# Semantic rows of the first layer's stacks: from DMA transfers to ScalarE copies

## The chip, the cores and the metric

The kernel runs on one core of one Trainium2 chip. The metric is the time of one execution on the device in microseconds (us), as the median of several runs; lower is better. In the profile PE is TensorE's matmuls, PEld its weight loads, DVE is VectorE, ACT is ScalarE, POOL is GpSimd, SP is the engine that issues most transfers. ACTq and SPq are the instruction queues of ScalarE and SP, in which a transfer's issue shows up.

## What is computed

Two cross-attention layers run one after the other on 16 sequences of 256 positions with 320 channels (20 heads of 16). Each attends to a context of 256 rows, of which the first 77 are text and the other 179 are image tokens in layer 0. The first layer (layer 0 in the code) is the one that the change touches. Cut to what matters:

```
logits     = q_h @ k_h^T * scale                    # per head, 77 text keys
text_out   = softmax(logits) @ v_h
scores     = q_h @ ip_k_h^T * scale                 # per head, 179 image keys
text_probs = softmax(q @ k_text^T * scale)          # all heads together: 77 columns
sem        = (text_probs @ text) @ ip^T * scale
fused      = scores + 0.5 * sem                     # the same sem in every head
ip_out     = (softmax(fused) * spatial_mask) @ ip_v_h
out        = (text_out + ip_out) @ Wout + bout + x
```

So the semantic term is a product of a 77-row matrix (text_probs, transposed) with a 77 x 179 matrix (half of text times ip), added to the scores of every head.

## The kernel before, in words

**Stacks.** The kernel adds the semantic term by stacking rows along the contraction dimension of one matmul. A stack is a pair of tiles Q and K, each 128 partitions x 4 heads x 256. There are four such pairs (`SIZES["NR"]`), used in turn by step k; a step is one group of four heads of one sequence, five steps a sequence, 80 steps in layer 0 (`NS`). Before the change rows 0 to 47 (`XROW` = 48) hold q and k in three parts of 16 rows (high halves and remainders of the numbers), rows 48 to 124 the 77 semantic rows, and rows 125 and 126 (`KS0` = 127) serve to subtract the row maxima: K holds there two rows of -1 (one for the text columns, one for the image columns), and Q the row maxima themselves. In K the semantic rows are zero for the 77 text columns (set once, by a memset).

**Filling a stack** is `stacks0` (L608 to L622). Four transfers go through the helper `dma`, which issues on SP (L82): part "K" and part "Q" bring 48 rows from DRAM (`kd<-kst` and `qd<-q` wrote them there); part "T" broadcasts `tph` (the transposed text probabilities, 77 x 256) to the four heads, and part "M" broadcasts the 77 x 179 matrix `M`. Parts T and M are done for groups 0 to 3 of a sequence only, because group 4 uses the same pair as group 0 and finds them there. The stack of step k + 4 (`LEAD`) is filled in step k, once the matmuls of step k that read the same pair are issued.

**A step of layer 0** is `slot0`. In order it asks for `maxima0` of step k + 1, the first half of `score0` of step k + 2, the first half of `turned0` of step k, `attend0` of step k - 1, and then the second halves of `score0` and `turned0`; between them stands work of other parts (projections of queries, keys and values, the close of a sequence), which a list of tasks with due times hands out. TensorE keeps this written order (`PINNED`). The order on ScalarE, VectorE, GpSimd and SP is made by the framework's scheduler in the loop; in the ramp before it (`begin`) all engines keep the written order.

**The maxima.** `score0` makes the scores of four heads (L649) and reduces them on VectorE to two maxima a head, over text (L650) and image columns (L651), into `mn`. `maxima0` turns `mn` with a matmul (L657), copies the result to `mt`, 8 rows x 256, on ScalarE (L659), and brings it into rows 125 and 126 of Q by one transfer for each head, issued on ScalarE (L661; on SP for the first two steps). `turned0` makes the scores again, transposed and with the maxima subtracted (L673), takes the exponential on ScalarE (L676) and multiplies on GpSimd by `rs`, a factor from the second-order part of the semantic term (L679). The second exponential of a step is ordered behind the issue of the next step's last maxima transfer. `values0` multiplies with the values (L709), and `settle0` normalizes.

**The semantic softmax** is `semantic0`, once a sequence: matmuls (L571), a copy on ScalarE (L573), the row maximum on VectorE, the exponential with its sum on ScalarE (L582), then the reciprocal (L585) and the scaling (L586) on VectorE, for two halves of 128 positions; then a transpose on TensorE (L590), and `tph` as a high half (L592, ScalarE) and a remainder (L593).

Of the kernel before, what the change touches and what calls it, by code (L numbers as in the profile page):

```python
# [9 lines left out]
FR = mybir.dt.float32r  # L10
AF = mybir.ActivationFunctionType
ALU = mybir.AluOpType
AX = mybir.AxisListType
# [4 lines left out]
S = 256  # L18
# [5 lines left out]
T0 = 77  # L24
# [7 lines left out]
KS0 = 127  # L32
KS1 = 50
XROW = 48
# [14 lines left out]
def xattn2(  # L49
# [27 lines left out]
    nc = tc.nc  # L77
    f = lambda ap: ap.bitcast(F32)
    mm = nc.tensor.matmul

    def dma(out, in_):
        nc.sync.dma_start(*(f(ap) if ap.dtype == FR else ap for ap in (out, in_)))  # L82
# [16 lines left out]
    def buf(tag, shape, dtype=F32, bufs=1, name=None):  # L99
        if tag in ("wB", "wD", "vr", "raw"):  # L100
            return sb.tile(shape, dtype, tag=tag, name=name or tag, bufs=bufs)
        size = 1
        for d in shape[1:]:
            size *= d
        if tag not in slots:
            slots[tag] = [0, dtype] + [const_tile([128, max(size, words.get(tag, 0))], f"{tag}_{i}", dtype) for i in range(bufs)]
        n, kind, *ring = slots[tag]
        assert kind == dtype and len(ring) == bufs, tag
        slots[tag][0] += 1
        t = ring[n % bufs][: shape[0], :size]  # L110
        names = "abcd"[: len(shape) - 1]
        if len(names) > 1:
            t = t.rearrange(f"p ({' '.join(names)}) -> p {' '.join(names)}", **dict(zip(names, shape[1:])))
        return t
# [4 lines left out]
    kd = [dram.tile([B // 2, 3, CP, 2, S], F32, name="kd0"), dram.tile([B, 3, CP, 1, S], F32, name="kd1")]  # L119
# [21 lines left out]
    def anchor(inst):  # L141
        anchors[inst.ins.engine] = inst
        return inst
# [120 lines left out]
    for i in range(SIZES["NR"]):  # L264
        nc.gpsimd.memset(f(ks[i]), 0.0)
        nc.gpsimd.memset(f(qs[i]), 0.0)
        dma(ks[i][XROW + T0 : KS0], ind0r.unsqueeze(1).to_broadcast([2, 4, S]))
    V0W, V1W = 17, 22
    vr = [buf("vr", [128, 3, H * V0W + 16], bufs=3) for i in range(3)]
    vcols = lambda v, w: v[:, :, : H * w].rearrange("p t (h e) -> p t h e", e=w)  # L270
# [268 lines left out]
    def stack_rows(d):  # L539
        return d.rearrange("r (d h) t -> (r d) h t", h=HP)  # L540
# [13 lines left out]
    def semantic0(b):  # L554

        qh, qd = get("q0", b)
        NT = 96
        kt = first_kt[0] if b == 0 else buf("kb", [128, 3, 2, NT], FR, name="kt")
        for s, r in ((0, 0), (1, 2)) if b else ():
            dma(kt[:, :, s], kd[0][b // 2, r].rearrange("(m p) b t -> p m b t", p=128)[:, :, b % 2, :NT])  # L560
        yield
        mh = get("m0t", b)

        tps = []
        for t in range(2):
            sf = bank()
            for k in range(3):
                qt = lambda h: qh[:, h, k, t * 128 : (t + 1) * 128]
                for h in range(2):
                    both = kt[:, k].rearrange("p s n -> p (s n)")  # L570
                    mm(sf[:, : 2 * NT], qt(h), both, start=k + h == 0, stop=k + h == 3)  # L571
            sp = buf("sp", [128, T0], bufs=2)
            nc.scalar.copy(sp, sf[:, NT : NT + T0])  # L573
            nc.vector.tensor_add(sp, sp, sf[:, :T0])
            mz = buf("mx", [128, 2], bufs=2)
            mx, zs = mz[:, 0:1], mz[:, 1:2]
            nc.vector.tensor_reduce(mx, sp, axis=AX.X, op=ALU.max)
            nc.vector.tensor_scalar_mul(mx, mx, -SCALE)
            tps.append((sp, mx, sp, zs))
            yield  # L580
        for sp, mx, tp, zs in tps:
            nc.scalar.activation(tp, sp, AF.Exp, bias=mx, scale=SCALE, accum_out=zs)  # L582
        yield
        for sp, mx, tp, zs in tps:
            nc.vector.reciprocal(zs, zs)  # L585
            nc.vector.tensor_scalar_mul(tp, tp, zs)  # L586
        yield
        tpp = bank()
        for t in range(2):
            nc.tensor.transpose(tpp[:T0, t * 128 : (t + 1) * 128], tps[t][2], ident)  # L590
        tph = buf("tph", [T0, 2, S], FR, bufs=2)
        nc.scalar.copy(tph[:, 0], tpp[:T0, :S])  # L592
        nc.vector.tensor_sub(tph[:, 1], tpp[:T0, :S], f(tph[:, 0]))  # L593
        yield

        rs = buf("rs", [128, 2, S], bufs=2)
        rp = bank().rearrange("p (t q) -> p t q", t=2)
        for t in range(2):
            mm(rp[:, t], mh[:, 0, t * 128 : (t + 1) * 128], tph[:, 1], start=True, stop=False)
            mm(rp[:, t], mh[:, 1, t * 128 : (t + 1) * 128], tph[:, 0], start=False, stop=True)  # L600
        nc.scalar.activation(rs, rp, AF.Exp, scale=SCALE)
        yield
        return qd, tph, rs, mh
# [4 lines left out]
    def stacks0(k, parts="KQTM"):  # L608
        b, g = divmod(k, NG)
        Q, K = QK[k] = qs[k % SIZES["NR"]], ks[k % SIZES["NR"]]  # L610
        hs = slice(4 * g, 4 * g + 4)
        for part in parts:
            if part == "K":
                dma(K[0:XROW], stack_rows(kd[0][b // 2][:, :, b % 2])[:, hs])
            elif part == "Q":
                dma(Q[0:XROW], stack_rows(get("q0", b)[1])[:, hs])
            elif g < SIZES["NR"]:
                tph, mh = get("s0", b)[1::2] if part == "T" else (None, get("m0t", b))
                if part == "T":
                    dma(Q[XROW : XROW + T0], tph[:, 0:1].to_broadcast([T0, 4, S]))  # L620
                else:
                    dma(K[XROW : XROW + T0, :, T0:], mh[:, 0:1, T0:].to_broadcast([T0, 4, S - T0]))  # L622


    def stacks1(k):
# [16 lines left out]
    def score0(k, t):  # L642
        Q, K = QK[k]
        if t == 0:
            maxes[k] = buf("mn", [128, 2, 4, 2], FR, bufs=2)
        mn = maxes[k]
        sp = scores()
        for h in range(4):
            mm(sp[:, h], Q[: XROW + T0, h, t * 128 : (t + 1) * 128], K[: XROW + T0, h], start=True, stop=True)  # L649
        nc.vector.tensor_reduce(mn[:, t, :, 0], sp[:, :, :T0], axis=AX.X, op=ALU.max)  # L650
        anchor(nc.vector.tensor_reduce(mn[:, t, :, 1], sp[:, :, T0:], axis=AX.X, op=ALU.max))  # L651

    def maxima0(k, queue=nc.scalar):
        Q, mn = QK[k][0], maxes[k]
        mp = bank()
        for t in range(2):
            mm(mp[:8, t * 128 : (t + 1) * 128], mn[:, t].rearrange("p h a -> p (h a)"), ident_r, start=True, stop=True)  # L657
        mt = buf("mt", [8, S], FR)
        nc.scalar.copy(mt, mp[:8, :S])  # L659
        for h in range(4):  # L660
            issues[k] = queue.dma_start(f(Q[XROW + T0 : KS0, h]), f(mt[2 * h : 2 * h + 2]))  # L661

    def turned0(k, t):

# [318 lines left out]
    def get(*key):  # L983
        while key not in results:
            step(key)
        return results[key]
# [209 lines left out]
```

## Time and profile before

| What | Value |
|---|---|
| Runs, us | 1663.47, 1673.33, 1674.31 |
| Median, us | 1673.33 |
| Span of the profiled execution (first to last instruction), us | 1663.4 |
| Its own time | not given beside the span; the lowest run is as long as the span |
| Mean granted TensorE clock | 0.974 |
| PE busy | 1533.5 us, 92% |
| DVE busy | 1317.2 us, 79% |
| ACT busy (without issuing transfers) | 877.7 us, 53% |
| POOL busy | 1202.2 us, 72% |
| Chain that ended last | PE 55%, DVE 18%, DMA 10%, POOL 4%, SPq 4% |
| Transfers of part T (`qs<-tph`) | 64 of 308 KB |
| Transfers of part M (`ks<-M`) | 64 of 215.4 KB |
| Transfers of the maxima in layer 0 (`qs<-mt`) | 312 on ACT's queue and 8 on SP's, 2 KB each |

How to read it: layer 0 takes the first half of the span, about as far as 750 us; layer 1 the rest. A row of the waits names the engine and line that waited, what it waited for, the total in us, how often, and the longest. In the groups of instructions the numbers after the bar are the busy time, the mean ns of one, and the idle time before them. In a timeline an entry such as [0.81 <-DMA qs<-mt] is the idle time before the instruction and what ended it.

### The profile page before, as it was taken

What the parts mean: (1) busy time and instruction counts of PE and PEld (TensorE: products, weight loads), DVE (VectorE), ACT (ScalarE), POOL (GpSimd) and SP (SyncE); (2) the same over time, 40 slices, a digit from 0 to 9 for tenths busy, and PEclk for the clock granted to TensorE, in tenths of its full rate; (3) what the DMA queues carried; (4) which work ended last, traced back from release to release, by engine and by line L of the source; (5) the groups of instructions that cost most, each with busy time, mean ns of one, the idle gap of its engine ahead of it and who ended that gap; (6) DMA issues with size and microseconds to landing.
All of it is one profiled execution on the core that took longest, in us unless ns stands there. A gap on an engine that the chain in (4) does not pass through costs nothing.

```text
span 1663.4 us, 35253 instructions
## 1 busy us (share of the span) xinstructions
PE 1533.5 (92%) x12666; PEld 1222.9 (74%) x12666; DVE 1317.2 (79%) x2484; ACT 877.7 (53%) x1865; POOL 1202.2 (72%) x1194
## 2 busy tenths in 40 slices
PE   7789999999999898789999999999999999999996
PEld 6677888787888786677677777777777777777754
DVE  5367676777776677867889889889888998899885
ACT  5344444444444445435656555655565556556563
POOL 3458787878787767767778777867876777777784
PEclk9899999999999899899999999999999999999998
DMA  7867777777776676655424342434243324332301
GB/s 219 218 196 212 200 215 197 211 202 213 198 220 194 192 203 185 159 178 153 147 66 129 106 128 90 133 106 129 85 131 113 120 89 131 117 105 82 115 17 43
DMA packets 247739, 247.43 MB, mean 149 GB/s; under 512 B 31050, under 2 KB 231468, under 8 KB 247564
## 3 DMA queue, kind: packets, MB, share of 16 engines
q1 hardware_dynamic: 245356, 243.87, 49.7%
q8 instruction: 101, 1.65, 0.4%
q10 hardware_dynamic: 2208, 1.30, 0.3%
q14 instruction: 74, 0.61, 0.1%
HBM read 121.21 MB, written 88.18 MB: 126 GB/s over the span
## 4 chain that ended last, share of the span: by engine, by line
PE 55%; DVE 18%; DMA 10%; POOL 4%; SPq 4%; issue 3%; ACT 3%; ACTq 0%; DVEq 0%; POOLq 0%
PE X L205 14%; PE X L814 12%; PE X L522 8%; PE P L709 5%; DMA qs<-qd 4%; SPq L82 4%; PE S L649 3%; DVE mn L781 3%; DVE wt L818 3%; PE T L673 3%; PE P L826 3%; PE T L775 2%; DVE wt L816 2%; PE P L828 2%; DVE ho L512 2%
## 5 line engine op out<-in xcount | busy, mean ns | idle before, releaser
L679 POOL TENSOR_TENSOR P<-P,rs 128x512 f32<-128x512 f32 x320 | 412.2, 1309 | 169.3 <-ACT P L676 169.0
L805 POOL TENSOR_TENSOR wt<-P,ctb 128x512 f32<-128x512 f32 x320 | 451.0, 1424 | 76.0 <-ACT ctb L804 75.6
L814 PE MATMUL X<-ctb,gm 128*128 128x512 f32 x1120 | 329.3, 412 | 2.5 <-DVE wt L816 2.5
L676 ACT ACTIVATE P<-T 128x512 f32<-128x512 f32 x320 | 176.1, 595 | 233.8 <-PE T L673 128.3
L786 ACT ACTIVATE P<-T 128x512 f32<-128x512 f32 x320 | 173.9, 597 | 138.8 <-PE T L775 137.4
L816 DVE TENSOR_TENSOR wt<-X,wt 128x512 f32<-128x512 f32 x320 | 215.3, 678 | 17.4 <-PE X L814 16.9
L804 ACT ACTIVATE ctb<-P 128x512 fp32r<-128x512 f32 x320 | 195.3, 632 | 61.5 <-PE X L814 60.8
L814 PEld LDWEIGHTS X<-ctb,gm 128*128 128x128 f32 x1120 | 189.6, 188 | 48.6 <-DVE wt L816 5.2
L781 DVE TENSOR_REDUCE mn<-S 128x4 fp32r<-128x1008 f32 x160 | 191.1, 1194 | 0.6 <-PE S L780 0.6
L651 DVE TENSOR_REDUCE mn<-S 128x4 fp32r<-128x716 f32 x160 | 142.6, 891 | 0.0
L673 PE MATMUL T<-qs,ks 127*128 127x256 f32 x640 | 112.5, 296 | 22.9 <-DVE tmp L726 9.9
L709 PE MATMUL P<-P,vr 128*32 128x256 f32 x1920 | 129.3, 405 | 0.0
L649 PE MATMUL S<-ks,qs 125*128 125x256 f32 x640 | 117.7, 308 | 11.7 <-DMA ks<-kd 4.6
L649 PEld LDWEIGHTS S<-ks,qs 125*128 125x128 f32 x640 | 88.7, 195 | 48.6 <-issue 38.4
L522 PE MATMUL X<-ho,wF 128*128 128x256 f32 x768 | 112.4, 289 | 6.7 <-DVE ho L512 2.9
L522 PE MATMUL X<-hq,wE 128*128 128x256 f32 x768 | 111.9, 289 | 5.8 <-ACT hq L511 3.1
L818 POOL TENSOR_TENSOR wt<-wt 128x512 f32<-128x512 f32 x80 | 103.3, 1292 | 14.8 <-DVE wt L816 14.7
L673 PEld LDWEIGHTS T<-qs,ks 127*128 127x128 f32 x640 | 93.0, 198 | 28.0 <-DVE tmp L726 11.9
L522 PEld LDWEIGHTS X<-ho,wF 128*128 128x128 f32 x768 | 103.0, 194 | 12.5 <-DVE ho L512 4.6
L522 PEld LDWEIGHTS X<-hq,wE 128*128 128x128 f32 x768 | 102.7, 194 | 11.4 <-POOL hq L512 5.2
L650 DVE TENSOR_REDUCE mn<-S 128x4 fp32r<-128x308 f32 x160 | 74.9, 468 | 44.1 <-PE S L649 43.6
L818 DVE TENSOR_TENSOR wt<-wt 128x512 f32<-128x512 f32 x80 | 106.1, 1326 | 2.1
(201 smaller groups left out, 2973.9 us busy)
## 6 DMA issues: line engine op xcount, KB each, us to landing
qd<-q SPq DMA_DIRECT2D x96, 384.0 KB
qs<-tph SPq DMA_DIRECT2D x64, 308.0 KB
kd<-kst SPq DMA_DIRECT2D x73, 256.0 KB
rawc<-in_cT_dram SPq DMA_DIRECT2D x60, 256.0 KB
qs<-qd SPq DMA_DIRECT2D x80, 192.0 KB
ks<-kd SPq DMA_DIRECT2D x80, 192.0 KB
ks<-kd SPq DMA_DIRECT2D x160, 96.0 KB
qs<-qd SPq DMA_DIRECT2D x160, 96.0 KB
```

The source lines that it names most:

```text
L205: last = mm(out, lhs(a, k), rhs(b, k), start=i == 0, stop=i == len(terms) - 1)
L522: mm(pp, w(s, k, slice(m * 128, (m + 1) * 128)), a[:, t], start=i == 0, stop=i == len(terms) - 1)
L649: mm(sp[:, h], Q[: XROW + T0, h, t * 128 : (t + 1) * 128], K[: XROW + T0, h], start=True, stop=True)
L673: mm(st[p][:, j], K[:KS0, 2 * p + j, t * 128 : (t + 1) * 128], Q[:KS0, 2 * p + j], start=True, stop=True)
L679: anchor(nc.gpsimd.tensor_mul(pt, pt, rs[:, t : t + 1].to_broadcast([128, 2, S])))
L709: mm(pv[32 * s : 32 * s + 32, o : o + S], v[:, vt, h : h + 32], P[k, s // 2][:, t, s % 2], start=vt < 2, stop=vt != 1,)
L781: anchor(nc.vector.tensor_reduce(maxes[k + 2][:, t], sp[:, :, :T1], axis=AX.X, op=ALU.max))
L804: nc.scalar.activation(R[k, u][:, t], P[k, u][:, t], AF.Copy, scale=0.5)
L805: anchor(nc.gpsimd.tensor_sub(W[k, u][:, t], P[k, u][:, t], f(R[k, u][:, t])))
L814: mm(yp, gm[:, gb], R[k, u][:, kt], start=i == 0, stop=i == len(blocks[n]) - 1)
L816: nc.vector.tensor_mul(w[:, n], yp, w[:, n])
L818: (nc.vector if u else nc.gpsimd).tensor_add(w[:, 0], w[:, 0], w[:, 1])
```

## The change

Three things are done in one edit, all in layer 0.

1. The semantic rows go to the head of the stack, rows 0 to 76, and q and k to rows 77 to 124. Parts T and M of `stacks0` are then written by ScalarE copies with a broadcast source in place of transfers. The maxima's rows stay where they are.
2. The maxima tile `mn` is laid out with the kind (text, image) ahead of the head, so that the eight rows of `mt` go into two partitions of Q in one transfer in place of four.
3. The scaling of the semantic softmax (L586) moves from VectorE to ScalarE.

```diff
-        dma(ks[i][XROW + T0 : KS0], ind0r.unsqueeze(1).to_broadcast([2, 4, S]))
+        dma(ks[i][KS0 - 2 : KS0], ind0r.unsqueeze(1).to_broadcast([2, 4, S]))
...
             nc.vector.reciprocal(zs, zs)
-            nc.vector.tensor_scalar_mul(tp, tp, zs)
+            nc.scalar.activation(tp, tp, AF.Copy, scale=zs)
...
             if part == "K":
-                dma(K[0:XROW], stack_rows(kd[0][b // 2][:, :, b % 2])[:, hs])
+                dma(K[T0 : T0 + XROW], stack_rows(kd[0][b // 2][:, :, b % 2])[:, hs])
             elif part == "Q":
-                dma(Q[0:XROW], stack_rows(get("q0", b)[1])[:, hs])
+                dma(Q[T0 : T0 + XROW], stack_rows(get("q0", b)[1])[:, hs])
...
                 if part == "T":
-                    dma(Q[XROW : XROW + T0], tph[:, 0:1].to_broadcast([T0, 4, S]))
+                    nc.scalar.copy(Q[:T0], f(tph[:, 0:1]).to_broadcast([T0, 4, S]))
                 else:
-                    dma(K[XROW : XROW + T0, :, T0:], mh[:, 0:1, T0:].to_broadcast([T0, 4, S - T0]))
+                    nc.scalar.copy(K[:T0, :, T0:], f(mh[:, 0:1, T0:]).to_broadcast([T0, 4, S - T0]))
...
-            maxes[k] = buf("mn", [128, 2, 4, 2], FR, bufs=2)
+            maxes[k] = buf("mn", [128, 2, 2, 4], FR, bufs=2)
...
-        nc.vector.tensor_reduce(mn[:, t, :, 0], sp[:, :, :T0], axis=AX.X, op=ALU.max)
-        anchor(nc.vector.tensor_reduce(mn[:, t, :, 1], sp[:, :, T0:], axis=AX.X, op=ALU.max))
+        nc.vector.tensor_reduce(mn[:, t, 0], sp[:, :, :T0], axis=AX.X, op=ALU.max)
+        anchor(nc.vector.tensor_reduce(mn[:, t, 1], sp[:, :, T0:], axis=AX.X, op=ALU.max))
...
-            mm(mp[:8, t * 128 : (t + 1) * 128], mn[:, t].rearrange("p h a -> p (h a)"), ident_r, start=True, stop=True)
+            mm(mp[:8, t * 128 : (t + 1) * 128], mn[:, t].rearrange("p a h -> p (a h)"), ident_r, start=True, stop=True)
...
-        for h in range(4):
-            issues[k] = queue.dma_start(f(Q[XROW + T0 : KS0, h]), f(mt[2 * h : 2 * h + 2]))
+        issues[k] = queue.dma_start(f(Q[KS0 - 2 : KS0]), f(mt))
```

## The prediction

> **What bounds the kernel now.** I read the busy times by stage first, then what TensorE waited for, then its granted clock, then two places in order of time. The stages, with the columns stretch, length, then PE, PEld, DVE, ACT and POOL busy (with counts), granted PE clock, DMA share, GB/s:
>
> ```profile
> 140.00:740.00 600.00, 548.11 (x4953) 464.63 (x4953) 429.63 (x954) 284.65 (x653) 448.50 (x419) 0.95 0.71 201
> 840.00:1663.40 823.40, 779.21 (x6096) 584.31 (x6094) 725.79 (x1209) 472.73 (x945) 610.05 (x627) 0.99 0.33 102
> ```
>
> The first row is layer 0 in its steady part, the second is layer 1, which the change leaves alone. In layer 0 TensorE is busy 548 of 600 us, so no cure of waits can bring more than 52 us there, plus what the clock gives (0.95 of full speed against 0.99). The DMA engines are 71% busy. What TensorE waited for from 140 to 800 us (us in total, times, longest):
>
> ```profile
> PE T L673 <- DMA qs<-mt: 8.8, 10, 1.5
> PE S L649 <- DMA ks<-kd: 4.6, 4, 1.4
> PE X L590 <- DVE sp L586: 3.2, 1, 3.2
> PE S L649 <- DMA qs<-qd: 2.7, 3, 1.6
> PE S L649 <- DMA qs<-tph: 0.8, 1, 0.8
> ```
>
> These five rows are what the change can reach: the row maxima (8.8), the stack's loads (4.6 + 2.7 + 0.8 = 8.1) and the softmax scaling (3.2), 20.1 us in all. The dearer part is the clock. The same columns as above, for the ramp and for five stretches in which a maxima wait falls:
>
> ```profile
> 56.00:72.00 16.00, 8.69 (x41) 7.94 (x39) 5.51 (x14) 6.40 (x15) 8.74 (x8) 0.57 0.91 237
> 148.00:156.00 8.00, 8.00 (x62) 6.11 (x63) 5.21 (x11) 3.61 (x11) 5.61 (x7) 0.79 0.86 216
> 228.00:236.00 8.00, 6.17 (x47) 4.51 (x44) 5.66 (x16) 4.58 (x13) 7.39 (x7) 0.79 0.93 272
> 312.00:320.00 8.00, 6.76 (x41) 4.69 (x42) 4.72 (x14) 3.43 (x11) 6.41 (x6) 0.58 0.96 241
> 396.00:404.00 8.00, 6.57 (x50) 4.90 (x51) 5.38 (x16) 3.77 (x12) 6.40 (x6) 0.79 0.91 246
> 480.00:484.00 4.00, 3.53 (x22) 3.16 (x25) 1.96 (x9) 2.53 (x8) 4.00 (x4) 0.58 0.85 213
> ```
>
> Time lost to the clock is PE busy times (1 - clock): 3.7 us in the ramp row, and 1.7 + 1.3 + 2.8 + 1.4 + 1.5 = 8.7 us in the other five. So each maxima wait is paid about twice: once as the wait, once as slow matmuls behind it.
>
> The Trainium skill, "TensorE: Matmul & The Clock Gate", Part 1, says that the clock falls to half after an idle window of some 3.4 us. The trace has it fall after shorter stops, because 8.8 us in ten waits is 0.9 us each and the clock in those rows is 0.58 to 0.79. By the rule these stops would not slow the clock, three quarters of the 8.7 us below would not come back, and the sum would be 17 us in place of 24.
>
> **The maxima: four transfers become one.** In order of time near 480 us (start, us, engine, line):
>
> ```profile
> 475.84 1.79 ACTq L661 DMA_DIRECT2D qs<-mt  x2
> 477.73 1.09 ACT L676 ACTIVATE P<-T 128x512 f32<-128x512 f32 x2 [3.89 <-PE X L657]
> 479.32 0.38 PE L673 MATMUL T<-qs,ks 127*128 127x256 f32 x1 [0.81 <-DMA qs<-mt]
> 480.47 0.64 PE L673 MATMUL T<-qs,ks 127*128 127x256 f32 x2 [0.77 <-DMA qs<-mt]
> ```
>
> The third and fourth transfer of one slot are issued from 475.84 to 477.63, the exponential stands behind them on ScalarE until 477.73, and TensorE's matmuls of the later heads start at 479.32 and 480.47, the last 2.84 us after the last issue. What can hold an issue is seen on the chain that ended last:
>
> ```profile
> 423.93 6.31 DMA kd<-kst
> 430.25 0.57 ACTq L661
> ```
>
> A maxima issue waited until a transfer that has nothing to do with it (the keys going to DRAM) had landed. Four issues a slot are four chances of that; the change leaves one, right behind the copy of the maxima. The wait of 8.8 us and the 8.7 us of clock are 17.5 us. I take three quarters, 13 us, because a single late issue can still hold all four heads; the ends are 0 (eight rows in one transfer land no sooner than the last of four did) and 17.5.
>
> **The instructions of ScalarE and of the SP queue.** Rows for durations (mean ns after the busy time; for transfers the minimum, median and maximum ns of an issue):
>
> ```profile
> L511 ACT CAST hq<-xq 128x768 fp32r<-128x768 f32 x21 | 17.6, 838 | 0.0
> L147 ACT CAST cta<-rawc 128x512 fp32r<-128x512 f32 x24 | 14.1, 629 | 9.8 <-DMA rawc<-in_cT_dram 9.7
> L573 ACT COPY sp<-X 128x77 f32<-128x77 f32 x32 | 6.5, 235 | 5.7 <-PE X L571 5.7
> L586 DVE TENSOR_SCALAR sp<-sp,mx 128x77 f32<-128x77 f32 x32 | 20.3, 635 | 0.7
> L661 ACTq DMA_DIRECT2D qs<-mt x312: 569/570/1203, 70.0 to 746.6; - x156
> L82 SPq DMA_DIRECT2D qs<-tph x54: 827/876/960, 145.9 to 708.6; - x54
> L82 SPq DMA_DIRECT2D ks<-M x70: 563/848/877, 146.8 to 759.3; - x70
> ```
>
> A cast costs (838 - 629) / 256 = 0.816 ns an element, so 1024 elements cost 838 + 209 = 1047 ns and 716 (4 times 179) cost 796 ns; that the source is read four times over should not matter, and no row shows it. Groups 0 to 3 of 16 batches make 64 copies of each kind: 64 x 1.047 + 64 x 0.796 = 118 us. The scaling adds 32 x about 0.3 = 10 us (the 77-wide copy takes 235 ns; reading the factor adds something). Gone are three quarters of 312 issues, 234 x 0.57 = 133 us. ScalarE's load is even: 128 us for 133 us. Its order is not, and that is the price. Half a slot of layer 0:
>
> ```profile
> 503.46 2.55 POOL L679 TENSOR_TENSOR P<-P,rs 128x512 f32<-128x512 f32 x2 [1.38 <-ACT P L676]
> 507.92 1.50 PE L709 MATMUL P<-P,vr 128*32 128x256 f32 x24
> 510.02 2.23 ACTq L661 DMA_DIRECT2D qs<-mt  x2
> 512.35 1.09 ACT L676 ACTIVATE P<-T 128x512 f32<-128x512 f32 x2 [3.99 <-PE X L205]
> 513.02 2.54 POOL L679 TENSOR_TENSOR P<-P,rs 128x512 f32<-128x512 f32 x2 [2.55 <-ACT P L676]
> 515.60 0.64 PE L709 MATMUL P<-P,vr 128*32 128x256 f32 x8
> ```
>
> The exponential goes to GpSimd and from there to the value matmuls (L709). GpSimd was done at 506.01 for matmuls at 507.92 (1.91 us to spare), and at 515.56 for matmuls at 515.60 (0.04): the cover is 1 us on average and sometimes nothing. Here two issues of 2.23 us stood in front of the exponential; after the change they are mostly gone and the two copies, 1.84 us, come free at the same moment (both wait for the matmuls that read the stack last, which the exponential waits for as well). If they go behind it, GpSimd starts some 1.7 us sooner, and what is late next is the copy out of PSUM and the next maxima behind the copies. I take a cost of 3 us, 0.05 us for each of 64 slots; the ends are a gain of 5 (the 133 less 128) and a loss of 56 (rival 1).
>
> On SP's queue 128 issues go, 64 x (0.876 + 0.848) = 110 us. In each of those slots the loads of K and Q, which stood behind them, are issued up to 1.7 us sooner; their waits were at most 1.4 and 1.6 us long. The bytes go too: 315 + 220 KB a slot, 54 times in the 600 us, 29 of some 121 MB. I take 6 of the 8.1 us; the ends are 0 and 8.1.
>
> **The scaling of the semantic softmax.** L586 leaves VectorE, where it took 635 ns, and goes behind the exponential on ScalarE, which must then wait for the reciprocal. The one wait that TensorE had for it was 3.2 us. I take 2; the ends are 3.2 and a loss of 3 (ScalarE held 0.1 us for VectorE, 32 times). **The layout of the maxima** (all text maxima, then all image maxima) costs nothing: the reductions read the same elements, and only write their four results side by side.
>
> **The ramp.** There the order is written by hand and SP issues back to back. First and last of the transfers that go or shrink, and what waits for them:
>
> ```profile
> 37.70 0.90 SPq L82 DMA_DIRECT2D qs<-tph  x1
> 51.25 2.56 SPq L661 DMA_DIRECT2D qs<-mt  x4
> 58.73 0.87 SPq L82 DMA_DIRECT2D ks<-M  x1
> 59.70 2.30 SPq L82 DMA_DIRECT2D kb<-kd  x2
> 65.28 2.00 PE L571 MATMUL X<-kb,q 128*128 128x192 f32 x8 [5.79 <-DMA kb<-kd]
> ```
>
> Between 37.70 and 59.70 there are six issues of qs<-tph and ks<-M, about 0.88 us each, and four of maxima, of which one stays: 5.3 + 1.9 = 7.2 us. So kb<-kd is issued up to 7.2 us sooner, and TensorE's wait of 5.79 us and a part of the 3.7 us of clock go. I take 6; the ends are 0 (the keys that kb reads are landed no sooner) and 9.5. ScalarE's copies there fall into gaps: from 56 to 72 us it is busy 6.4 of 16.
>
> **The sum.** 13 + 6 + 2 + 6 - 3 = 24 us. The page's span:
>
> ```profile
> span 1663.4 us, 35253 instructions
> ```
>
> The three runs shown are 1663.47, 1673.33 and 1674.31; the page does not give the execution's own time beside the span, and the span is as long as the lowest run, 10 us under the median. From the span the sum gives 1639.4; I put it against the median, 1673.3 - 24 = 1649 us.
>
> **Rivals.** First, slower: the copies stand in front of the exponentials. If in each of the 64 slots the pair (1.84 us) delays GpSimd, with 0.98 us of cover on average, TensorE is 0.87 us late, 56 us in all; against 27 us of gains that is +29, 1702 us. It decides from 27 / 64 = 0.42 us a slot. For it: ScalarE's order in the loop is the scheduler's, and the cover of 0.04 us. Against it: ScalarE's total load is no larger, and what stood there before was as long.
>
> Second, within 1%: the merged transfer brings nothing. One transfer with eight rows lands when the last of four did (2.84 us after its issue, whatever the number), the clock dips stay because other waits cause them, and only 6 + 2 + 6 - 3 = 11 us are left: 1662. For it: the waits in the rows are small one by one, and TensorE is busy 91% in any case. Against it: the exponential itself stands behind the issues. The Trainium skill, "DMA: Bandwidth & Descriptors", section "Issuing engines are not separate DMA queues", speaks for this rival: it says that the time to initiate a DMA is usually small beside the transfer. Here the trace disagrees in size: 0.57 us an issue, and 2.23 us for two at 510.02.
>
> Third, faster than I say: all ends at their best, 17.5 + 8.1 + 3.2 + 9.5 + 5 = 43, so 1630 us.
>
> **How the numbers follow.** Forecast 0.50 (own range 1636 to 1656), third rival 0.08, second 0.25, first 0.17. Differences under 1% are about what a measurement of this kernel can't tell from none; 1% below the median is 1656.6. So faster 0.50 + 0.08 = 0.58, same 0.25, slower 0.17. The range goes from 1627, the third rival with a little to spare, to 1678, which holds the second rival and the mild form of the first (0.5 us a slot) and leaves most of the first outside.
>
> **What would show it.** Right: no T L673 waits for qs<-mt, one ACTq issue of L661 a slot, clock near 1.00 at the five places, PE L571 waiting under 2 us in the ramp, the DMA share of layer 0 near 0.6, copies of 1.0 and 0.8 us behind the exponentials. Wrong: POOL L679 waiting for ACT P L676 longer than before, PE P L709 waiting for POOL, or a single maxima transfer that still lands late.

## The result and the profile after

The changed kernel takes 1632.91 us (median of four runs, 1631.75 to 1634.92) against 1671.02 before (four runs, 1663.47 to 1674.31). The ratio is 0.9775, 95% interval 0.9751 to 0.98: 38 us faster, where the forecast was 24. The profiled execution of the changed kernel took 1631.75 us, of which 1630.0 are span. From its page, the span and the chain that ended last:

```profile
span 1630.0 us, 34838 instructions
...
PE 69%; DVE 19%; issue 4%; POOL 3%; ACT 3%; DMA 2%; SPq 0%; ACTq 0%; DVEq 0%; POOLq 0%
```

Transfers have left the chain: 10% before, 2% now, and SP's queue 4% before, 0% now.

The stages of the changed kernel, with the columns of the prediction (stretch, length, PE, PEld, DVE, ACT, POOL busy, granted PE clock, DMA share, GB/s): layer 0, layer 1, the ramp, and nearly the whole of layer 0.

```profile
140.00:740.00 600.00, 566.62 (x5213) 483.64 (x5206) 451.19 (x972) 388.17 (x829) 473.38 (x445) 0.97 0.59 162
840.00:1630.00 790.00, 747.82 (x5859) 560.39 (x5858) 697.04 (x1161) 455.01 (x908) 585.41 (x604) 0.99 0.34 104
56.00:72.00 16.00, 11.42 (x76) 8.87 (x77) 5.35 (x16) 7.72 (x21) 12.40 (x10) 0.79 0.71 166
72.00:740.00 668.00, 627.65 (x5751) 536.73 (x5751) 495.25 (x1066) 430.05 (x916) 518.01 (x486) 0.97 0.58 159
```

The same last stretch of the kernel before:

```profile
72.00:740.00 668.00, 609.38 (x5498) 518.62 (x5499) 474.96 (x1051) 317.11 (x728) 495.19 (x461) 0.95 0.70 199
```

In the same 668 us TensorE works 18.3 us more, at 0.97 of full speed in place of 0.95, so the work at full speed goes from 609.38 x 0.95 = 579 to 627.65 x 0.97 = 609 us: 30 us more (26 where the clock is taken in stretches of 4 us, as in the part on the clock below). Layer 0 ends about that much sooner. The transposes that close its 80 steps show where (count, minimum, median and maximum ns, first and last start), before and after:

```profile
L720 DVE STREAM_TRANSPOSE nt<-P x80: 674/717/719, 76.2 to 766.8; 128x512 f32<-128x512 f32 x80
```

```profile
L719 DVE STREAM_TRANSPOSE nt<-P x80: 673/717/719, 71.9 to 734.1; 128x512 f32<-128x512 f32 x80
```

The first step ends 4.3 us sooner (the ramp), the last 32.7 us sooner. Between them a step takes (766.8 - 76.2) / 79 = 8.74 us before and (734.1 - 71.9) / 79 = 8.38 after: 0.36 us a step. The spans differ by 33.4, so layer 1 gave 0.7. This first and last start is the yardstick of all experiments below.

The 0.36 us is a mean, and the gain is not spread evenly. The first 51 of the same closes, before and after:

```profile
L720 DVE STREAM_TRANSPOSE nt<-P x51: 697/717/719, 76.2 to 503.2; 128x512 f32<-128x512 f32 x51
```

```profile
L719 DVE STREAM_TRANSPOSE nt<-P x51: 697/717/719, 71.9 to 493.2; 128x512 f32<-128x512 f32 x51
```

The 50 steps from the first to the 51st close take 427.0 us before and 421.3 after, 5.7 less. The 29 steps behind them take 766.8 - 503.2 = 263.6 and 734.1 - 493.2 = 240.9, 22.7 less. All ten waits of `T L673` for the maxima, and all five places at which the prediction counted lost clock, lie in the first 50 steps. (The span of the profiled execution before, 1663.4 us, is some 8 us under the median of that kernel's runs, so its parts are good to about that.)

What TensorE waited for in the first 860 us of the changed kernel (total, times, longest):

```profile
PE X L522 <- DVE ho L512: 7.0, 6, 1.2
PE X L205 <- ACT wA L147: 6.4, 3, 5.1
PE X L657 <- DVE mn L651: 5.7, 5, 2.8
PE X L522 <- ACT vr L343: 5.6, 7, 0.9
...
PE X L522 <- ACT mt L659: 3.3, 5, 0.7
...
PE X L571 <- DMA kb<-kd: 2.5, 1, 2.5
```

Of the transfers' rows only `kb<-kd` is left. The waits for `mt`, `ks` and `qs` of the prediction's list are gone. In their place stand copies of ScalarE that come late (`vr`, `mt`). Summed over the rows of 72 to 740 us by what ended the wait, TensorE waited before 23.0 us for transfers, 2.5 for ScalarE and 30.4 for VectorE (58.3 in all), and after 2.5, 13.7 and 21.0 (39.8 in all). TensorE waits for ScalarE more than before; VectorE is still the larger of the two. By place: from 72 to 500 us the waits were 25.2 before (19.7 of them for transfers) and 23.1 after (2.5 for transfers, 11.5 for VectorE, 7.8 for ScalarE), so others took the place of those that were cured. From 500 to 740 us they were 33.2 before, 28.0 of them for VectorE, and 16.6 after, 9.4 for VectorE. The two largest rows of the kernel before there, which the prediction did not list:

```profile
PE T L673 <- DVE tmp L726: 9.9, 2, 5.9
PE X L657 <- DVE mn L651: 5.8, 4, 2.7
```

Why VectorE is late less there is not shown. The merged maxima alone (e1 below) bring the 28.0 us to 13.8 and the copies alone (e2) to 15.1; the scaling alone (e3) leaves 27.4.

The copies are as long as forecast, and the scaling takes 0.35 us for the "about 0.3" of the sum (busy time, mean ns):

```profile
L620 ACT CAST qs<-tph 77x1024 fp32r<-77x1024 f32 x64 | 66.6, 1043 | 0.0
L622 ACT CAST ks<-M 77x716 fp32r<-77x716 f32 x64 | 50.7, 794 | 0.0
L586 ACT ACTIVATE sp<-sp,mx 128x77 f32<-128x77 f32 x32 | 10.7, 354 | 1.6 <-DVE mx L585 0.9 <-ACT mt L659 0.7
```

The copies stand where the forecast put them: 59 of the 64 pairs come right behind an exponential. One of them (start, us, engine, line):

```profile
507.94 1.09 ACT L675 ACTIVATE P<-T 128x512 f32<-128x512 f32 x2 [2.20 <-PE T L672]
508.91 1.04 ACT L620 CAST qs<-tph 77x1024 fp32r<-77x1024 f32 x1
509.85 0.79 ACT L622 CAST ks<-M 77x716 fp32r<-77x716 f32 x1
...
510.76 0.36 ACT L659 CAST mt<-X 8x256 fp32r<-8x256 f32 x1
...
511.15 0.62 ACTq L660 DMA_DIRECT2D qs<-mt  x1
511.17 1.21 PE L522 MATMUL X<-ho,wF 128*128 128x256 f32 x8 [0.66 <-ACT mt L659]
```

The copy of the maxima (510.76) comes after both copies, and TensorE waits 0.66 us for it: the copies are late work for the next maxima, as the prediction said, but it is a real price. SP's queue waits less as well. It waited for older transfers before it could issue, from 140 to 740 us, in the kernel before (total, times, longest), largest rows:

```profile
SPq L82 <- DMA ks<-kd: 46.2, 34, 3.3
SPq L82 <- DMA ks<-M: 24.1, 17, 2.9
SPq L82 <- DMA qs<-tph: 20.9, 7, 3.8
SPq L82 <- DMA kd<-kst: 14.8, 17, 2.5
```

In the changed kernel the largest such row is

```profile
SPq L82 <- DMA x1d<-xc: 9.0, 9, 2.1
```

All such rows together are 140.5 us in 105 waits before and 12.9 us in 14 after. They are no price of the large transfers, though: the merged maxima alone bring them to 35.1 us with all 128 large transfers in place (e1), the copies alone to 44.4 (e2), and with 128 large transfers put back beside the copies they are 16.0 (e8).

### The profile page after: what moved, and what is told of

The parts are those of the page before. It is cut to its first block, busy times and chain, and to the rows that moved or that the text cites. A ratio compares the mean times of both kernels' runs of the same rounds, so it can differ in the third digit from the quotient of the medians.

```text
span 1630.0 us, 34838 instructions
## 1 busy us (share of the span) xinstructions
PE 1521.6 (93%) x12666; PEld 1215.2 (75%) x12666; DVE 1310.1 (80%) x2452; ACT 979.6 (60%) x2025; POOL 1201.4 (74%) x1194
## 4 chain that ended last, share of the span: by engine, by line
PE 69%; DVE 19%; issue 4%; POOL 3%; ACT 3%; DMA 2%; SPq 0%; ACTq 0%; DVEq 0%; POOLq 0%
PE X L205 18%; PE X L813 12%; PE X L522 10%; PE P L708 7%; PE S L649 5%; PE T L672 4%; DVE mn L780 3%; DVE wt L817 3%; PE P L825 3%; PE T L774 2%; DVE wt L815 2%; PE P L827 2%; DVE ho L513 2%; DVE ho L512 2%; DVE kb L500 2%
## 5 line engine op out<-in xcount | busy, mean ns | idle before, releaser
L678 POOL TENSOR_TENSOR P<-P,rs 128x512 f32<-128x512 f32 x320 | 415.6, 1321 | 147.1 <-ACT P L675 145.8
L205 PE MATMUL X<-cta,wA 128*128 128x252 f32 (+1 forms) x720 | 98.4, 282 | 10.5 <-ACT wA L147 6.2
L672 PE MATMUL T<-qs,ks 127*128 127x256 f32 x640 | 104.5, 286 | 0.0
```

The costliest lines, as they stand in the source:

```text
L205: last = mm(out, lhs(a, k), rhs(b, k), start=i == 0, stop=i == len(terms) - 1)
L678: anchor(nc.gpsimd.tensor_mul(pt, pt, rs[:, t : t + 1].to_broadcast([128, 2, S])))
```

## The experiments

Two questions were open. Which part carries the gain: do the parts add up, as the forecast's sum supposes, or do they need each other? And what do the copies cost: the 3 us of the forecast, or as much as rival one made of them? The kernel before was timed beside each group of experiments on the same chip. In the diffs below "-" and "+" are against the kernel named. Differences between two experiments are those of the medians; worked out from the two ratios they come out up to 4 us apart, and so less than about 8 us is not read as a cause.

### The parts alone

**One maxima transfer, nothing else** (e1, against the kernel before; the layout of `mn` goes with it):

```diff
-        for h in range(4):
-            issues[k] = queue.dma_start(f(Q[XROW + T0 : KS0, h]), f(mt[2 * h : 2 * h + 2]))
+        issues[k] = queue.dma_start(f(Q[KS0 - 2 : KS0]), f(mt))
```

> The kernel before with the maxima in one transfer alone; the semantic rows still come by transfers on SP and the softmax scaling stays on VectorE. Theory A (the issues on ScalarE: four maxima issues a step stand in front of the exponential, and any of them can be held): most of the gain is here, about 20 of the 38 us, 1651 us, and no T matmul waits for qs<-mt. Theory B (the SP queue and the bytes: 128 large transfers less): little, under 8 us, over 1663 us, because the one transfer is held as the four were. Theory C (VectorE: the scaling behind other work late in layer 0): under 8 us as well.

Measured: 1656.41 us against 1671.55, ratio 0.9916 (0.9894 to 0.9938). It brings 15 us by the medians, 14 by the ratio; the term of the sum was 13. TensorE's waits for transfers, 72 to 740 us:

```profile
PE S L649 <- DMA qs<-qd: 10.2, 6, 2.3
PE X L571 <- DMA kb<-kd: 5.3, 1, 5.3
PE X L657 <- DMA x1d<-xc: 3.5, 1, 3.5
PE S L649 <- DMA ks<-kd: 1.3, 1, 1.3
```

The waits for `qs<-mt` (8.8 us) are gone, but the load of Q, which had 2.7 us, now has 10.2. With the maxima in time, the stack's load is what comes late. Waits for transfers fell only from 23.0 to 20.3 us. Up to the 51st close the loop takes 423.7 us, 3.3 less than before; 8.9 us of the gain lie behind it, where the kernel before had no wait of `T L673` for the maxima.

**The copies, nothing else** (e2, against the kernel before; q and k move to rows 77 to 124 with them):

```diff
-                    dma(Q[XROW : XROW + T0], tph[:, 0:1].to_broadcast([T0, 4, S]))
+                    nc.scalar.copy(Q[:T0], f(tph[:, 0:1]).to_broadcast([T0, 4, S]))
...
-                    dma(K[XROW : XROW + T0, :, T0:], mh[:, 0:1, T0:].to_broadcast([T0, 4, S - T0]))
+                    nc.scalar.copy(K[:T0, :, T0:], f(mh[:, 0:1, T0:]).to_broadcast([T0, 4, S - T0]))
```

> The kernel before with the semantic rows written by ScalarE copies, the maxima still in four transfers, the scaling on VectorE. Theory A: ScalarE now has four issues and two copies a step in front of the exponential, so no gain or a loss, 1668 to 1690 us. Theory B: most of the gain, 20 us or more, 1650 us or less, and the SP queue no longer waits for its own older transfers. Theory C: under 10 us.

Measured: 1664.24 us against 1671.55, ratio 0.9957 (0.994 to 0.9975): 7 us. The profiled execution, 1671.23 us, is the slowest of its ten. Here the waits for the stack's loads are gone and those for the maxima stay:

```profile
PE T L673 <- DMA qs<-mt: 8.9, 7, 2.1
PE X L571 <- DMA kb<-kd: 4.2, 1, 4.2
```

**The scaling, nothing else** (e3, against the kernel before):

```diff
-            nc.vector.tensor_scalar_mul(tp, tp, zs)
+            nc.scalar.activation(tp, tp, AF.Copy, scale=zs)
```

> The kernel before with the softmax scaling on ScalarE alone. My prediction had 2 us for it. Theory C: 12 us or more, all of it after step 60, 1659 us or less. Theories A and B: within 3 us of the kernel before.

Measured: 1667.46 us against 1671.55, ratio 0.9987 (0.9969 to 1.0006): no difference that this measurement shows.

**All but the scaling** (e4, against the changed kernel: the line of e3 the other way round):

> The changed kernel with the scaling left on VectorE, so the maxima in one transfer and the copies together. Theories A and B: 1633 to 1637 us. Theory C: 1645 us or more.

Measured: 1642.39 us against 1671.55, ratio 0.9848 (0.9814 to 0.9881). It is 9.5 us slower than the changed kernel, though the scaling alone brings nothing. TensorE's waits differ little (38.7 us against 39.8); the time lost to the clock from 72 to 740 us, summed over stretches of 4 us, is 21.3 us against 16.5. What the scaling does there stays open; every edit lets the scheduler set ScalarE's and VectorE's order anew, and a few us may be that.

**All but the maxima** (e5, against the changed kernel; the old layout of `mn` goes with it):

```diff
-        issues[k] = queue.dma_start(f(Q[KS0 - 2 : KS0]), f(mt))
+        for h in range(4):
+            issues[k] = queue.dma_start(f(Q[XROW + T0 : KS0, h]), f(mt[2 * h : 2 * h + 2]))
```

> The changed kernel with the maxima in four transfers again; copies and scaling as changed. Theory A (the four issues on ScalarE and the waits for them): the loss is the larger part, 20 us or more, 1653 us or over, with T matmuls waiting for qs<-mt again and time lost to the clock. Theory B (SP queue and bytes): under 8 us lost, 1641 us or less, since one issue or four then find the transfer slots free.

Measured: 1669.55 us against 1669.05, ratio 1.0 (0.9983 to 1.0018). The whole gain is gone: the merged transfer that alone is worth 14 us is worth 37 here. First and last close of a step, busy times and TensorE's waits for transfers, 72 to 740 us:

```profile
L720 DVE STREAM_TRANSPOSE nt<-P x80: 675/716/719, 71.5 to 768.3; 128x512 f32<-128x512 f32 x80
```

```profile
72.00:740.00 668.00, 612.51 (x5452) 519.10 (x5455) 463.41 (x1017) 413.49 (x873) 489.91 (x457) 0.95 0.53 150
```

```profile
PE T L673 <- DMA qs<-mt: 7.1, 5, 1.8
PE X L571 <- DMA kb<-kd: 3.1, 1, 3.1
```

The ramp keeps its gain (71.5), but a step takes 8.82 us, more than before. ScalarE is busy 413 of 668 us and issues four transfers a step on top (0.57 us each in the prediction's row), so ScalarE has more to do ahead of the exponentials than in either of the two kernels. GpSimd's wait for it in this kernel, and in the changed one, 72 to 740 us, goes with that (148.1 us in the kernel before):

```profile
POOL P L679 <- ACT P L676: 158.5, 100, 5.3
```

```profile
POOL P L678 <- ACT P L675: 127.9, 92, 5.3
```

**All but the copies** (e12, against the changed kernel; rows back to the order of before, the transfers on SP):

```diff
-                    nc.scalar.copy(Q[:T0], f(tph[:, 0:1]).to_broadcast([T0, 4, S]))
+                    dma(Q[XROW : XROW + T0], tph[:, 0:1].to_broadcast([T0, 4, S]))
...
-                    nc.scalar.copy(K[:T0, :, T0:], f(mh[:, 0:1, T0:]).to_broadcast([T0, 4, S - T0]))
+                    dma(K[XROW : XROW + T0, :, T0:], mh[:, 0:1, T0:].to_broadcast([T0, 4, S - T0]))
```

> The changed kernel with the semantic rows left to transfers on SP: the maxima in one transfer and the scaling on ScalarE, no copies. It gives what the copies are worth against the transfers that they replace. From the maxima alone at 1656 and the changed kernel at 1633: if the scaling does nothing by itself (as it did alone), 1654 to 1657 us and the copies are worth 22 us beside their own price of 29; if the scaling also pays once the maxima are out of the way (as it did with the copies, 9 us), 1645 to 1648 us.

Measured: 1657.88 us against 1670.26, ratio 0.9921 (0.9891 to 0.9951), 25 us slower than the changed kernel. TensorE's waits for transfers, 72 to 740 us:

```profile
PE S L649 <- DMA qs<-qd: 22.8, 12, 3.1
PE X L571 <- DMA kb<-kd: 4.7, 2, 4.4
PE X L657 <- DMA x1d<-xc: 3.6, 1, 3.6
```

The loads of Q, behind the broadcasts on SP's queue, come late for 22.8 us in all, against 2.7 before and none in the changed kernel. The gains of all seven kernels:

| Parts | us | Gain by the ratio, us |
|---|---|---|
| maxima (e1) | 1656.41 | 14 |
| copies (e2) | 1664.24 | 7 |
| scaling (e3) | 1667.46 | 2, not told from 0 |
| copies and scaling (e5) | 1669.55 | 0 |
| maxima and scaling (e12) | 1657.88 | 13 |
| maxima and copies (e4) | 1642.39 | 25 |
| all three | 1632.91 | 38 |

The single gains make 0.0084 + 0.0043 + 0.0013 = 0.0140 of 1671, 23 us; the whole is 0.0225, 38 us. The difference, 14 us, is twice what the half widths of the four intervals (0.0022, 0.0018, 0.0019, 0.0025) make as independent errors, 7 us. So the parts do not add up. But maxima and copies without the scaling bring 25 us, within the error of 14 + 7; the excess stands in the kernels with the scaling, which by the ratios brings 2 us alone, takes 7 from the copies (e5 against e2) and adds 12 to the other two together. Waits do come out from behind others: the load of Q goes from 2.7 us to 10.2 with the maxima merged (e1), and to 22.8 when the scaling is moved too (e12), while VectorE's share of TensorE's waits falls from 25.3 to 15.0 us and the time stays the same. How much of the 14 us such hidden waits make is not shown.

The closes tell more (us; one profiled execution of each kernel):

| Kernel | First close | 50 steps to the 51st | 29 steps to the last |
|---|---|---|---|
| before | 76.2 | 427.0 | 263.6 |
| maxima (e1) | 77.5 | 423.7 | 254.7 |
| copies (e2) | 73.7 | 446.7 | 247.8 |
| copies and scaling (e5) | 71.5 | 445.9 | 250.9 |
| maxima and scaling (e12) | 78.9 | 431.5 | 249.9 |
| maxima and copies (e4) | 71.4 | 425.1 | 243.7 |
| all three | 71.9 | 421.3 | 240.9 |
| all three, no rows written (e6, below) | 72.7 | 392.9 | 237.7 |

In the first 50 steps the copies make the kernel slower as long as ScalarE also issues four maxima transfers a step (e2, e5), and not when it issues one (e4, all three). Between e5 and the changed kernel the last closes lie 34 us apart, and 25 of them come up in these 50 steps. In the last 29 steps the maxima alone bring 9 us, the copies alone 16 and both together 20, so there they overlap rather than help each other.

### What the copies cost and what the transfers cost

**The copies left out** (e6, against the changed kernel; it leaves the semantic term out of the scores):

```diff
-                    nc.scalar.copy(Q[:T0], f(tph[:, 0:1]).to_broadcast([T0, 4, S]))
+                    pass
...
-                    nc.scalar.copy(K[:T0, :, T0:], f(mh[:, 0:1, T0:]).to_broadcast([T0, 4, S - T0]))
+                    pass
```

> Leaves out the two ScalarE copies of each stack, so the semantic rows stay zero and the semantic term is missing from the scores; all else as in the changed kernel. This gives the price of the copies. My prediction had 3 us, so 1630 us. Rival: the copies delay ScalarE's other work (the copies out of PSUM, which TensorE waits for, are new in the waits of the changed kernel at about 10 us) and cost 8 us or more: 1625 us or less.

Measured: 1604.09 us against 1669.05, ratio 0.961 (0.9583 to 0.9638). Writing the rows with ScalarE costs 29 us, not 3.

```profile
L719 DVE STREAM_TRANSPOSE nt<-P x80: 668/717/719, 72.7 to 703.3; 128x512 f32<-128x512 f32 x80
```

```profile
72.00:740.00 668.00, 639.63 (x5974) 548.62 (x5966) 507.74 (x1106) 358.65 (x828) 540.39 (x505) 0.98 0.59 163
```

```profile
POOL P L678 <- ACT P L675: 99.6, 86, 7.5
```

The ramp is no shorter (72.7), but a step takes 7.98 us against 8.38 on average: 0.4 us, next to the 1.84 us that a pair of copies lasts. Nearly all of it lies in the first 50 steps (7.86 us against 8.43); the last 29 take 8.20 against 8.31. GpSimd waits 28 us less for the exponential, and TensorE's waits for ScalarE fall from 13.7 to 6.2 us and for VectorE from 21.0 to 15.8. From 72 to 500 us TensorE waits 6.9 us in place of 23.1, and the granted clock is 1.00 in place of 0.98. The rows that shrink or go are those of `vr` and `mt`, which are ScalarE's, and of `ho`, which ScalarE casts (L511) before VectorE works on it (L512). For GpSimd's product TensorE had waited only 0.9 us. This kernel also drops the stacks' dependence on `tph` and `M`, so the 29 us hold the copies' time and what waiting for their sources costs; no run separates the two. With nothing written into those rows of the stacks the matmuls multiply other data; whether a part of the clock (0.98 in place of 0.97) comes from that can't be told here.

Taken with e12, the cost of writing the rows by transfers was 1657.88 - 1604.09 = 54 us, of which the copies give 29 back. The next two put transfers back beside the copies, into spare DRAM that nobody reads: as many as left, first of 2 KB (e7), then of the old size (e8).

```diff
                     nc.scalar.copy(Q[:T0], f(tph[:, 0:1]).to_broadcast([T0, 4, S]))
+                    dma(spare()[:2, 0], tph[:2, 0])
...
                     nc.scalar.copy(K[:T0, :, T0:], f(mh[:, 0:1, T0:]).to_broadcast([T0, 4, S - T0]))
+                    dma(spare()[:2, 0], mh[:2, 0])
```

> The changed kernel with two transfers of 2 KB on SP beside each pair of copies, 128 in all, from the same sources into a scratch that nobody reads. It brings back the number of transfers and SP's issue time but not the bytes. Theory N (number: each transfer on SP's queue delays the ones behind it): 5 us or more lost, 1638 us or over, and SP waiting for its own older transfers. Theory W (weight: bytes and long landings): within 3 us of the changed kernel.

Measured: 1635.89 us against 1669.05, ratio 0.9814 (0.9766 to 0.9861): 3 us above the changed kernel, within its interval. By the ratios it is 6 us. The number of transfers and their issue time on SP are a small part of the cost at most.

And the old size (e8, against the changed kernel, in the same two places):

```diff
+                    dma(spare()[:T0], tph[:, 0:1].to_broadcast([T0, 4, S]))
...
+                    dma(spare()[:T0, :, T0:], mh[:, 0:1, T0:].to_broadcast([T0, 4, S - T0]))
```

> The same with the full 308 and 215 KB of each (into DRAM, not into the stack), 128 in all, so number, issue time and bytes are back while the rows themselves still come by ScalarE. Theory W: 8 us or more lost, 1641 us or over, with K and Q loads late again. Theory N: the same loss as with the small ones, within 3 us. If neither loses anything, what the transfers cost was only that the stack's rows themselves landed late.

Measured: 1657.63 us against 1669.05, ratio 0.9937 (0.9916 to 0.9958): 25 us above the changed kernel. The large transfers cost this much even where nobody reads what they write. (They go to DRAM here, and to the stacks before; what that changes was not measured.) The ramp and the closes of the steps:

```profile
56.00:72.00 16.00, 8.26 (x42) 7.34 (x41) 3.56 (x8) 5.35 (x13) 6.18 (x5) 0.70 0.92 266
```

```profile
L728 DVE STREAM_TRANSPOSE nt<-P x80: 673/716/718, 79.3 to 756.7; 128x512 f32<-128x512 f32 x80
```

In the ramp the DMA share is 0.92 again (0.71 in the changed kernel, 0.91 before), the first step ends at 79.3 in place of 71.9, and a step takes 8.57 us. This is 25 of the 54; the rest is bound up with stacks that wait for these transfers and the loads behind them (the 22.8 us of e12; here no such wait is in the rows), which is argued and was not measured by itself.

### Where the copies stand

**The maxima issued by SP** (e9), and the exponential no longer ordered behind their issue on ScalarE:

```diff
-    def maxima0(k, queue=nc.scalar):
+    def maxima0(k, queue=nc.sync):
...
-            if t and k + 1 in issues:
-                queued(exp, issues[k + 1])
```

> The changed kernel with the one maxima transfer issued on SP's queue in every step, and the exponential no longer ordered behind it. Theory S (ScalarE's time, copies and issues alike, is the price in layer 0: taking three of four issues off, some 117 us of 0.57 us issues over layer 0 to step 79, gave 36 us, and leaving the copies out 29 us of 118, so 0.25 to 0.3 us for each us): 47 us less on ScalarE give 12 to 14 us, 1620 us. Rival P (place: only what stands in front of the exponential counts, and behind SP's other transfers the maxima come late): 1633 us or more, with T matmuls waiting for qs<-mt.

Measured: 1643.88 us against 1671.32, ratio 0.9832 (0.9793 to 0.987): 11 us slower than the changed kernel, with no wait for `qs<-mt` and an issue of 0.62 us a step less on ScalarE. The theory that the time follows ScalarE's occupation, about 0.25 to 0.3 us for each us on it (e5: 37 us for 3 x 0.57 x 78 = 133 us; e6: 29 for 117), is not borne out here.

**M's rows by VectorE** (e10):

```diff
-                    nc.scalar.copy(K[:T0, :, T0:], f(mh[:, 0:1, T0:]).to_broadcast([T0, 4, S - T0]))
+                    nc.vector.tensor_copy(K[:T0, :, T0:], f(mh[:, 0:1, T0:]).to_broadcast([T0, 4, S - T0]))
```

> The changed kernel with the copies of M on VectorE, those of tph still on ScalarE. Theory S: 51 us less on ScalarE give 12 to 15 us, less what VectorE's copies cost, 1620 to 1626 us. Rival V (VectorE, 75% busy in layer 0, is as tight as ScalarE, and its copies delay the reductions of the scores): no gain, 1631 us or more.

Measured: 1651.7 us against 1671.32, ratio 0.9894 (0.9869 to 0.992): 19 us slower than the changed kernel. The copy is longer on VectorE, GpSimd's multiply is longer too (1321 ns in the changed kernel), and TensorE now waits for VectorE, 35.1 us from 72 to 740 against 21.0:

```profile
L622 DVE CAST ks<-M 77x716 fp32r<-77x716 f32 x64 | 69.0, 1080 | 0.0
L678 POOL TENSOR_TENSOR P<-P,rs 128x512 f32<-128x512 f32 x320 | 430.7, 1368 | 135.8 <-ACT P L675 116.6 <-DMA kb<-kd 19.0
```

```profile
PE X L522 <- DVE ho L512: 12.4, 7, 2.0
```

**The copies half a step later** (e11): the loads of K and Q stay where they were, the copies move to the second half of the step.

```diff
-            yield lambda: stacks(k + LEAD)
+            yield lambda: stacks(k + LEAD, "KQ")
...
+        if k != 1:
+            yield lambda: stacks(k + LEAD, "TM")
```

> The changed kernel with the two copies asked for after the other work between two steps, and no longer right behind the second exponential; the number is the same. Theory S: the amount counts and not the place, within 5 us of the changed kernel's 1633. Rival P: the copies are in the way of the copies out of PSUM, and later they cost less: 1625 us or less.

Measured: 1639.81 us against 1671.32, ratio 0.9815 (0.9799 to 0.9831): 7 us slower than the changed kernel, about the least that is read here. The copies are late work for others there. TensorE's waits, 72 to 740 us:

```profile
PE X L205 <- ACT mt L659: 8.4, 6, 1.4
...
PE X L590 <- ACT sp L586: 6.5, 2, 3.5
```

Its waits for ScalarE go up to 23.9 us (13.7 in the changed kernel), those for VectorE down to 15.1. Neither theory met its number. No version that computes the whole was faster than the changed kernel.

## Why the prediction was right, and where its sum was not

**Direction: right. Mechanism: right where it was named, but most of the gain lies elsewhere.** The waits for the maxima and for the stack's loads are gone, the issue on ScalarE is one a step, the DMA share of layer 0 is 0.59 (forecast near 0.6), and the copies stand behind exponentials. The ramp gave 4.3 us of its 6. But the 50 steps that hold the cured waits for the maxima gained 5.7 us net, and the 29 steps behind them 22.7. There TensorE had waited 28.0 us for VectorE, of which the sum priced one row of 3.2 and put the rest at nothing, and now waits 9.4. So it is in part luck that the time, 1633, lies in the range, 16 us under the forecast: the rows' transfers (54 us against 6 + 6) and the rows' copies (29 against 3) were both priced too low, and these errors partly cancel. That it lies next to the third rival (1630) is chance as well, because that rival has the copies gain 5 us.

**The maxima, 13 us: right alone by number, by luck, and wrong as a term.** Alone they bring 14 us (e1), but in the first 50 steps, where all of the 13 was priced, e1 gains 3.3, and 8.9 come later. On top of the other two parts they bring 37 (e5). The step that failed is that each part was priced from the waits of the kernel before. There a wait shows only as far as no other wait ends later; e1 shows the load of Q come out from behind the maxima (2.7, then 10.2 us), and e2 and e5 the maxima stay when only the loads are cured. The sum also let four issues and two copies trade places on ScalarE, us for us; e5 shows what both together do there: 445.9 us for the first 50 steps against 421.3.

**What leaves with the transfers, 6 + 6 us: mis-sized.** The gross is 54 us (e12 less e6). Number and bytes, with no reader, make 25 of it (e8), the number alone 3 (e7); how the rest comes about is not shown. The prediction bounded the term by the waits that it could see in TensorE's rows, 8.1 us. The ramp's share of 6 us was right in place and about in size: the wait for `kb<-kd` at 65 us is gone, and the first step ends 4.3 us sooner than before and 7.0 sooner than in e12 (78.9). All kernels without the large transfers end the first step between 71.4 and 73.9 us, all five with them (before, e1, e3, e8, e12) between 76.2 and 79.3, so it is the transfers' leaving, and the merged maxima have no part in it (e1: 77.5).

**The price of the copies, 3 us: mis-sized; it is 29** (e6). The place was right, behind the exponential, and so was the next thing late, the copy of the maxima behind the copies. The step that failed is "0.05 us for each of 64 slots": it set the copies against the issues that leave, us for us. Measured by themselves the copies cost 0.4 us a step on average, half of what rival one took for its 56 us. That rival's time (1702) fell. Of its mechanism a part shows: GpSimd waits 28 us less for the exponentials without the copies. But its path to TensorE does not, since TensorE waits 0.9 us for GpSimd in the changed kernel; what goes in e6 is the waits for `vr`, `mt` and `ho` and the slow clock.

**The scaling, 2 us: not told from that alone** (e3), 9.5 us on top of the rest (e4), unexplained.

**The clock: in part.** By the two rows of 72 to 740 us the loss is 609.38 x 0.05 = 30 us before and 627.65 x 0.03 = 19 after; summed over stretches of 4 us it is 24.2 and 16.5, so 7.7 us come back. The prediction counted three quarters of 8.7 within its 13 and called the clock the dearer part, though its own rows give 8.7 + 3.7 = 12.4 us of clock against 20.1 of waits. In its five stretches the clock is now 1.00. What is left stands elsewhere: 0.86 from 124 to 132 us and 0.87 from 448 to 456, behind waits of 0.88 us for `vr` and 1.2 and 0.6 for `ho`. Of the 7.7 us the merged maxima alone bring only 3.6 (e1: 20.6). The Trainium skill, "TensorE: Matmul & The Clock Gate", Part 1, has the clock at half after at least one idle window of about 3.4 us; this trace disagrees, because in the prediction's five stretches the clock was 0.58 to 0.79 behind waits of at most 1.5 us, and the loss fell when such waits were cured. That longer waits for other things were cured in the same kernels, and gave a part of the 7.7, isn't separated.

**Rival two (nothing from the merged transfer) fell:** the merged transfer alone brings 14 us (e1), and its one issue takes 0.62 us on ScalarE. The rule of the Trainium skill that it leaned on, "DMA: Bandwidth & Descriptors", section "Issuing engines are not separate DMA queues", that initiation is usually small beside the transfer, agrees with e7, where 128 more issues on SP cost 3 us. It does not cover e5, where 3 x 78 more on ScalarE, an engine with work of its own in the same queue, cost 37 together with the waits for four transfers.

**What stays open:** why VectorE is late less behind 500 us, how much of the excess over the sum of the parts is hidden waits, why e9 and e11 are slower than the changed kernel, and how the scaling comes to its 9.5 us. In each of these kernels the scheduler orders ScalarE's stream anew, so these differences mix the edit with the order, and no run separates the two.

## What to carry to other kernels

A wait in the profile is a price only for the state in which it was measured: when a buffer waits for two late transfers, cure both in mind before you price either, and expect that curing one alone moves the wait to the other. A total that agrees with a term of the sum does not show that the term was right: look where in time the gain lies (here 5.7 us in the steps where most of it was priced and 22.7 behind them). A queue's own waits are not a price either (SP's fell from 140.5 to 35.1 us in e1 with all large transfers in place). And work moved to an engine that feeds the critical loop has a price even when that engine is 60% busy and the work stands behind the urgent instruction: here 0.4 us a step on average for copies of 1.84 us.

## What the runs showed of the hardware

A copy on ScalarE whose source is one row block read four times over costs the same as a plain one: 1043 and 794 ns, against 1047 and 796 worked out from plain casts. The same 77 x 716 cast takes 1080 ns on VectorE, and GpSimd's multiply in the same kernel goes from a mean of 1321 to 1368 ns. The issue of one transfer with eight 1 KB rows takes 0.621 us on ScalarE's queue, little more than the 0.570 of one with two rows. Adding 128 transfers of 2 KB to SP's queue moved the time by 3 us, within the interval, and adding 128 of 215 to 308 KB, which nothing reads, by 25. At five places of the kernel before, the granted clock was 0.58 to 0.79 over 4 to 8 us, behind waits of TensorE of at most 1.53 us.
